# Layer 1 of the last two quarters emitted in turn

## The chip, the core and the metric

The kernel runs on one core of a Trainium2 chip. The metric is the device time of one launch in microseconds, as a median over runs. A profiled execution of the same program gives a span (first to last instruction) and the granted clock of TensorE. Engines: PE is TensorE, DVE is VectorE, ACT is ScalarE, POOL is GpSimd, SP issues most DMAs.

## The reference, cut to what matters

Two transformer layers on 1024 tokens (32 sequences of 32) of width 256, in float32. Each `_ref` is one block, and four residual sums join them:

```python
x = x + _L0_attn_ref(_L0_cond_ref(x, ...), ...)     # a mixing per sequence, then attention in 16 heads
x = x + _L0_ffn_ref(_L0_cond2_ref(x, ...), ...)     # gated feed-forward with low-rank adapters, then a second one
x = x + _L1_attn_ref(_L1_cond_ref(x, ...), ...)     # attention with a scale per sequence, then a linear-memory read
x = x + _L1_ffn_ref(_L1_cond2_ref(x, ...), ...)     # attention over a paged cache, then a mixture of 16 experts
```

The change is in the third line. `_L1_cond_ref` projects q, k and v, scales q, takes a causal softmax within each sequence of 32, multiplies by v and by `Wo`. `_L1_attn_ref` then forms `sigma_q = elu(q) + 1` from its own projection of that, and for each of four memory banks `sigma_q @ memories / clip(sigma_q . memory_norms)`; the banks are summed with softmax weights and multiplied by a last `Wo`. The block behind it begins with projections of q, k and v from the new x, an RMS norm of each head and a rotation by position; the new k and v are written into the paged cache before it is read.

## The kernel before

The 1024 tokens are worked on in four quarters of 256 (`NQ = 4`), with features on the partitions: a tile of a quarter is 128 x 2 x 256[...]. Stages in order: the layer 0 attention of each quarter; the feed-forwards of quarter 0; then, by the loop of lines 879 to 882, `layer1(q)` followed by `feed_forward(q + 1)`, which needs nothing of `layer1(q)`; `layer1(3)` comes last and has no feed-forward after it. Then weights of the last stages are loaded (lines 886 to 900), the paged attention gathers its rows (line 921, `kv<-rows_d`), and the experts follow.

The order in which the lines are written is not the order of the instructions: a scheduler places every instruction in its engine's queue, so that `layer1(q)` and `feed_forward(q + 1)` come out mixed with each other.[...] What may be open at the same time is set by tile pools. In PSUM: `mm` has two banks (projections), `tr` two, `sc` one (scores and norms), `ff` three (feed-forward alone). In SBUF each tag has its own buffers: `x1` four and `res` four (one a quarter), `QT`, `KT` and `AV` two each, `V` and `y` one each, `kb`, `sm`, `PT`, `th` and `h` two each.

`layer1(q)` is a chain. `mha` makes q, k and v (three banks of `mm` in turn, helper `products`, whose matmuls all have line 177), spreads V into the block-diagonal tile `vblk` (sixteen small copies, lines 393 and 395, half on DVE and half on ACT), and for each of two groups of 128 tokens: spreads K into `kb` (402), multiplies by q (409), adds the mask, takes the softmax (417 to 427), transposes (430), copies to `PT` (432), multiplies by `vblk` (436) and copies into `AV` (443). Then follow `Wo` and the copy to `cT` (779), the `lq` product and its `elu + 1` on DVE and ACT (786 to 788), the norms (791) and their reciprocal `rn` (799 to 801), the spread of `rn` to all rows by `esel` (811, 64 rows high) times `sq` (812, tile `t4`), the memories `mblk` and the copy to `comb` (817), the `lo` product, and `x3` (821). Last come k and v of the next block, rotated, written to DRAM by a DMA in SP's queue (846), and q, rotated into `qall`. `rotated` is a row of DVE operations with a Square and a Sqrt on ACT.

The gathers of line 921 wait until every row of `rows_d` is written. The tile `ew` (6 MB of expert weights, 895) lies in the place of the feed-forwards' weights; its load waits for the last of their products, `f_w_down`.

Of the kernel before, what the change touches and what calls it, by code (L numbers as in the profile page):

```python
# [18 lines left out]
F32 = mybir.dt.float32  # L19
# [5 lines left out]
P = 128  # L25
B, S, D = 32, 32, 256
NT = B * S
NG = NT // P
CH = 512
NCH = NT // CH  # L30

NQ, QG = 4, 2
QN = QG * P
# [88 lines left out]
def tile_layers(ctx: ExitStack, tc: tile.TileContext, i: dict, out: bass.AP):  # L122
    nc = tc.nc
    v, s, g_, te = nc.vector, nc.scalar, nc.gpsimd, nc.tensor
# [79 lines left out]
    with (  # L204
# [9 lines left out]
        def bank(pool=mm, tag="mm"):  # L214
            return pool.tile([P, 2, QN], F32, tag=tag, name=tag)

        def tok(tag, bufs=2, shape=(P, 2, QN)):
            return qp.tile(list(shape), F32, tag=tag, name=tag, bufs=bufs)

        late = {}
# [15 lines left out]
        with (  # L238
# [4 lines left out]
            for q in range(NQ):  # L243
                t = xp.tile([P, QG, D], F32, name=f"x0{q}")
# [49 lines left out]
            wa = {k: load_w(wp, i[f"L0_attn_W{k}"], f"wa_{k}") for k in "qkvo"}  # L294
# [37 lines left out]
            x0T, zT = [], []  # L332
# [34 lines left out]
                    s.copy(x0T[q][:, :, js], pt[:, 2:])  # L367


        def mha(zq, w, q_out, k_out, v_out):  # L370


            QT, KT, V, AV = tok("QT"), tok("KT"), tok("V", 1), tok("AV")
            for dst, k, put in ((QT, "q", q_out), (KT, "k", k_out)):
                ps = bank()
                products([(ps[:, m], ktiles(w[k], m, zq)) for m in range(2)])
                put(dst, ps)
            ps = bank()
            products(
                [  # L380
                    (ps[:, j], [(zq[:, k, j * P : (j + 1) * P], w["v"][:, k, :]) for k in range(2)])
                    for j in range(QG)
                ]
            )
            v_out(V, ps)

            V4 = V.rearrange("p g (hg h d) -> p g hg h d", hg=4, h=4)
            for b4 in range(4):
                for h4 in range(4):
                    dst = vblk[32 * h4 : 32 * h4 + 32, :, b4, :, 16 * h4 : 16 * h4 + 16]  # L390
                    src = V4[32 * b4 : 32 * b4 + 32, :, :, h4, :]
                    if h4 % 2:
                        v.tensor_copy(dst, src)  # L393
                    else:
                        s.copy(dst, src)
            for j in range(QG):
                js = slice(j * P, (j + 1) * P)
                ps = sc.tile([P, CH], F32, tag="sc", name="sc")
                for m in range(2):

                    kb = sp.tile([P, 4, 8, 32], F32, tag="kb", name="kb")
                    v.tensor_tensor(  # L402
                        kb,
                        KT[:, m, js].rearrange("p (b k) -> p b k", b=4).unsqueeze(2).broadcast_to([P, 4, 8, 32]),
                        m8.unsqueeze(1).unsqueeze(3).broadcast_to([P, 4, 8, 32]),
                        ALU.mult,
                    )
                    for b4 in range(4):
                        te.matmul(  # L409
                            ps[32 * b4 : 32 * b4 + 32, m * 256 : (m + 1) * 256],  # L410
                            lhsT=QT[:, m, j * P + 32 * b4 : j * P + 32 * b4 + 32],
                            rhs=kb[:, b4].rearrange("p h k -> p (h k)"),
                            start=True,
                            stop=True,
                        )
                sm = sp.tile([P, 16, 32], F32, tag="sm", name="sm")
                v.tensor_tensor(  # L417
                    sm, ps.rearrange("p (h k) -> p h k", k=32), C("causal").unsqueeze(1).broadcast_to([P, 16, 32]), ALU.add
                )
                mx = sp.tile([P, 16], F32, tag="mx", name="mx")  # L420
                v.tensor_reduce(mx, sm, AX.X, ALU.max)  # L421
                v.tensor_tensor(sm, sm, mx.unsqueeze(2).broadcast_to([P, 16, 32]), ALU.subtract)
                s.activation(sm, sm, AF.Exp)
                su = sp.tile([P, 16], F32, tag="su", name="su")
                v.tensor_reduce(su, sm, AX.X, ALU.add)
                v.reciprocal(su, su)
                v.tensor_tensor(sm, sm, su.unsqueeze(2).broadcast_to([P, 16, 32]), ALU.mult)
                pt = tr.tile([P, 4, P], F32, tag="tr", name="tr")
                for hg in range(4):
                    te.transpose(pt[:, hg], sm[:, 4 * hg : 4 * hg + 4, :].rearrange("p h k -> p (h k)"), ident)  # L430
                PT = sp.tile([P, 4, P], F32, tag="PT", name="PT")
                s.copy(PT, pt)
                av = tr.tile([P, 4, P], F32, tag="tr", name="tr")
                for b4 in range(4):
                    for hg in range(4):
                        te.matmul(  # L436
                            av[64 * (hg % 2) : 64 * (hg % 2) + 64, hg // 2, 32 * b4 : 32 * b4 + 32],
                            lhsT=vblk[:, j, b4, hg, :],
                            rhs=PT[:, hg, 32 * b4 : 32 * b4 + 32],
                            start=True,  # L440
                            stop=True,
                        )
                s.copy(AV[:, :, js], av[:, :2])
            return AV


        x1T = []
        for q in range(NQ):
# [9 lines left out]
            def v_out(dst, ps):  # L458
                v.tensor_tensor(dst, ps, bv.unsqueeze(1).broadcast_to([P, QG, D]), ALU.add)

            AV = mha(zT[q], wa, q_out, k_out, v_out)
            x1T.append(tok("x1", 4))
            ps = bank()
            products([(ps[:, m], ktiles(wa["o"], m, AV)) for m in range(2)])
# [298 lines left out]
        esel = C("esel", 64).rearrange("p (n a c) -> p n a c", n=4, a=2)  # L763


        def layer1(q):
            def q_out(dst, ps):
                v.tensor_tensor(
                    dst.rearrange("p m (b t) -> p m b t", t=S),
# [2 lines left out]
                    ALU.mult,  # L772
                )

            AV = mha(x2T[q], wa1, q_out, s.copy, s.copy)
            cT = tok("AV")
            ps = bank()
            products([(ps[:, m], ktiles(wa1["o"], m, AV)) for m in range(2)])
            s.copy(cT, ps)


            sq = tok("QT")
            ps = bank()
            products([(ps[:, m], ktiles(lq, m, cT)) for m in range(2)])
            e = sp.tile([P, 2, QN], F32, tag="sm", name="e")
            v.tensor_scalar(e, ps, 0.0, None, ALU.min)
            s.activation(e, e, AF.Exp)
            v.scalar_tensor_tensor(flat(sq), flat(ps), 0.0, flat(e), ALU.max, ALU.add)
            pn = sc.tile([P, CH], F32, tag="sc", name="sc")
            for m in range(2):  # L790
                te.matmul(
                    pn[32 * m : 32 * m + 32, :QN],
# [6 lines left out]
            v.tensor_scalar(rn, pn[:64, :QN], 1e-6, None, ALU.max)  # L799
            v.reciprocal(rn, rn)  # L800
            v.tensor_scalar(rn, rn, wcol, None, ALU.mult)
            comb = tok("KT")
            pc = bank()
            sums = []
            for m in range(2):
                pairs = []
                t4 = sp.tile([P, 4, QN], F32, tag="kb", name="t4")
                for b2 in range(2):
                    ps = bank()
                    for a in range(2):  # L810
                        te.matmul(ps[:, a], lhsT=esel[:, 2 * b2 + a, m, :], rhs=rn, start=True, stop=True)  # L811
                    v.tensor_tensor(
                        t4[:, 2 * b2 : 2 * b2 + 2], ps, sq[:, m].unsqueeze(1).broadcast_to([P, 2, QN]), ALU.mult
                    )
                sums.append((pc[:, m], [(mblk[:, m, bnk, :], t4[:, bnk]) for bnk in range(4)]))
            products(sums)
            s.copy(comb, pc)
            ps = bank()
            products([(ps[:, m], ktiles(lo, m, comb)) for m in range(2)])
            x3 = x3T[:, :, q * QN : (q + 1) * QN]  # L820
            done = v.tensor_tensor(x3, ps, x2T[q], ALU.add)
# [13 lines left out]
                v.tensor_copy(at[:, :, 4], ps[:, B : B + NG])  # L835


            gs = slice(QG * q, QG * q + QG)
            kvw = tok("V", 1, (P, QG, D))
            ps = bank()  # L840
            xg = [[x3[:, k, j * P : (j + 1) * P] for k in range(2)] for j in range(QG)]
            products([(ps[:, j], [(xg[j][k], wqkv[:, k, D:]) for k in range(2)]) for j in range(QG)])
            s.copy(kvw[:, :, P:], ps[:, :, P:])
            kd = kvw[:, :, :P].rearrange("p g (h a d) -> a p g h d", a=2, d=16)
            rotated(ps[:, :, :P].rearrange("p g (h d) -> p g h d", d=32), 4, 1, gs, [(kd[0], kd[1])])
            nc.sync.dma_start(new_rows[:, gs, :], kvw)
            ps = bank()
            products([(ps[:, j], [(xg[j][k], wqkv[:, k, :D]) for k in range(2)]) for j in range(QG)])
            qd = qall[:, gs].rearrange("p g h k (a d) -> h a p g k d", a=2)
            rotated(ps.rearrange("p g (h d) -> p g h d", d=32), 8, 0, gs, [(qd[h, 0], qd[h, 1]) for h in range(2)])  # L850

        def rotated(x, nh, j, gs, dst):


            shape = [P, QG, nh, 32]

            def tile_(tag):
                t = sp.tile([P, CH], F32, tag=tag, name="r" + tag)
                return t[:, : QG * nh * 32].rearrange("p (g h d) -> p g h d", g=QG, h=nh)

            sq = tile_("sm")
# [14 lines left out]
                v.tensor_tensor(dst0, ak[:, :, :, :16], bk_[:, :, :, 16:], ALU.subtract)  # L876
                v.tensor_tensor(dst1, ak[:, :, :, 16:], bk_[:, :, :, :16], ALU.add)

        for q in range(NQ):
            layer1(q)  # L880
            if q + 1 < NQ:
                x2T.append(feed_forward(q + 1))


    with tc.tile_pool(name="w1", bufs=1, reuse_waits="tile") as wp:
# [455 lines left out]
```

## Time and profile before

| | us |
|---|---|
| median of 3 runs | 724.82 (724.69 to 726.23) |
| profiled execution, own time | 742.99 |
| its span | 741.1 |
| PE busy in the span | 596.4 (80%) |
| DVE, ACT, POOL busy | 375.9, 182.9, 188.4 |
| mean granted clock of PE | 0.895 of full |
| last feed-forward ends | 440.2 |
| last rows of k and v issued | 501.5 |
| first gather of the paged attention | 504.55 |

Times on the axis of the span are from the first instruction. A busy PE counts matmuls whose ends are modelled, and each float32 matmul of the program shows as two records. The rows of the views name a line, an operation and its tiles without buffer numbers: `mm<-res,wb_q` is a matmul from a `res` tile and a weight into a bank of `mm`.

### The profile page before, as it was taken

To read this page: it belongs to the slowest core of one execution; us is meant where nothing else is said; L and a number is where in the kernel's file an instruction comes from. 1 tells how busy PE (TensorE), PEld (TensorE's weight loads), DVE (VectorE), ACT (ScalarE), POOL (GpSimd) and SP (SyncE) were. 2 spreads that over 40 slices of the span, in tenths; PEclk is the share of its full clock that TensorE was granted. 3 is DMA by queue.
4 is the path that set the end of the run, shared out by engine and by line. 5 is a ranking of instruction groups with operands and counts; after the bars stand their busy time and mean duration, and the time that the engine had idled before them with its cause. 6 is when DMAs were issued, how large, how long until landed. Compare 5 with 4: busy or idle time off the path is not lost.

```text
span 741.1 us, 9080 instructions
## 1 busy us (share of the span) xinstructions
PE 596.4 (80%) x3246; PEld 457.5 (62%) x3246; DVE 375.9 (51%) x874; ACT 182.9 (25%) x490; POOL 188.4 (25%) x274
## 2 busy tenths in 40 slices
PE   2649899997999989999899994674388899249990
PEld 1426677784877858788588882452266657136660
DVE  4583584699445364333734227223177747115553
ACT  1132222213212122210222103011266643102220
POOL 6213333204694000000000000005456200624541
PEclk9877899998899999999899996675599999759996
DMA  6984354300700000000000036003212000223325
GB/s 197 252 298 127 107 134 129 113 13 2 219 15 14 1 1 1 1 14 1 0 2 0 15 121 261 1 1 106 64 58 72 23 0 1 86 75 114 117 61 170
DMA packets 37452, 55.35 MB, mean 75 GB/s; under 512 B 8906, under 2 KB 29536, under 8 KB 36576
## 3 DMA queue, kind: packets, MB, share of 16 engines
q1 hardware_dynamic: 27549, 37.62, 15.9%
q0 software_dynamic: 5904, 15.40, 7.6%
q10 hardware_dynamic: 3955, 1.75, 0.9%
q8 instruction: 26, 0.43, 0.2%
q14 instruction: 18, 0.15, 0.1%
HBM read 38.56 MB, written 18.17 MB: 77 GB/s over the span
## 4 chain that ended last, share of the span: by engine, by line
PE 48%; issue 27%; DVE 15%; POOL 4%; DMA 3%; ACT 2%; another core or an unknown queue 1%; POOLq 0%; SPq 0%; ACTq 0%; DVEq 0%
PE ff L177 26%; PE mm L177 13%; POOL ys_d L1247 4%; DVE kb L402 4%; PE tr L436 3%; PE mm L811 3%; DVE vblk L393 2%; PE tr L430 1%; DVE sm L417 1%; DMA y<-ys_d 1%; PE sc L409 1%; PE mm L346 1%; DVE mx L421 1%; DMA adi<-in_itok_B 0%
## 5 line engine op out<-in xcount | busy, mean ns | idle before, releaser
L921 POOL DMA_INDIRECT kv<-rows_d,at x40 | 38.7, 968 | 283.6 <-DMA sh_g<-in_L_ffn_sWg 273.0
L501 DVE SCALAR_TENSOR_TENSOR th<-th,ff 128x512 f32<-128x512 f32 x32 | 21.9, 683 | 63.5 <-ACT th L500 63.5
L560 POOL COPY rr<-raw 88x256 f32<-88x256 f32 x64 | 27.9, 467 | 80.0 <-DMA rows_d<-rr 40.8
L409 PE MATMUL sc<-kb,QT 128*32 128x256 f32 x256 | 24.5, 459 | 23.2 <-DVE kb L402 12.3
L402 DVE TENSOR_TENSOR kb<-KT,con 128x1024 f32<-128x1024 f32 x32 | 38.7, 1227 | 8.2 <-ACT KT L456 4.5
L1247 POOL DMA_INDIRECT ys_d<-yb,xb x31 | 30.6, 986 | 44.5 <-DVE yb L1245 43.0
L177 PE MATMUL ff<-x,w_g 128*128 128x256 f32 x128 | 39.7, 429 | 0.0
L1232 PE MATMUL gu<-ew,xT 128*128 x124 | 34.4, 400 | 2.7 <-issue 2.7
L500 ACT ACTIVATE th<-ff 128x512 f32<-128x512 f32 x32 | 19.1, 596 | 69.4 <-PE ff L177 66.5
L177 PE MATMUL ff<-x,w_u 128*128 128x256 f32 x128 | 35.1, 385 | 0.0
L177 PEld LDWEIGHTS ff<-x,w_g 128*128 128x128 f32 x128 | 27.5, 219 | 6.1 <-issue 1.2
L987 PE MATMUL po<-PT,kv 128*128 128x256 f32 x64 | 18.6, 415 | 15.3 <-ACT PT L984 15.3
L177 PE MATMUL ff<-y,f_w_gate 128*128 128x256 f32 x128 | 30.9, 379 | 0.0
L177 PE MATMUL ff<-y,f_w_up 128*128 128x256 f32 x128 | 30.9, 379 | 0.0
L177 PE MATMUL ff<-h,d_Wd 128*128 128x256 f32 x128 | 30.1, 381 | 0.0
L1226 PE MATMUL xt<-ident,xb 128*128 128x128 f32 x62 | 11.9, 290 | 21.8 <-DMA xb<-xs_d 21.7
L502 DVE SCALAR_TENSOR_TENSOR h<-th,ff 128x512 f32<-128x512 f32 x32 | 21.7, 680 | 15.2 <-PE ff L177 14.9
L409 PEld LDWEIGHTS sc<-kb,QT 128*32 128x32 f32 x256 | 5.5, 116 | 37.7 <-DVE kb L402 19.3
L177 PE MATMUL ff<-h,f_w_down 128*128 128x256 f32 x128 | 28.3, 379 | 0.0
L969 ACT ACTIVATE sm<-sm,mx 128x160 f32<-128x160 f32 x64 | 26.7, 418 | 5.5 <-DVE mx L967 4.4
L1232 PEld LDWEIGHTS gu<-ew,xT 128*128 128x128 f32 x124 | 23.1, 199 | 7.0 <-issue 3.2
L955 PE MATMUL sc<-KT,qz 128*128 128x160 f32 x128 | 25.7, 339 | 1.4 <-issue 1.1
(334 smaller groups left out, 1346.0 us busy)
## 6 DMA issues: line engine op xcount, KB each, us to landing
ew<-in_L_ffn_W SPq DMA_DIRECT2D x1, 6144.0 KB
rows_d<-rr SPq DMA_DIRECT2D x32, 176.0 KB
xs_d<-none SPq DMA_DIRECT2D x1, 3999.0 KB
xb<-xs_d SPq DMA_DIRECT2D x31, 129.0 KB
x<-in_x SPq DMA_DIRECT2D x4, 256.0 KB
w_g<-in_L_cond_Wg SPq DMA_DIRECT2D x1, 1024.0 KB
w_u<-in_L_cond_Wu SPq DMA_DIRECT2D x1, 1024.0 KB
d_Wd<-in_L_cond_Wd SPq DMA_DIRECT2D x1, 1024.0 KB
```

What stands on the lines that cost most here:

```text
L177: mm_ = te.matmul(ps, lhsT=a, rhs=b, start=j == 0, stop=j == len(pairs) - 1)
L402: v.tensor_tensor(kb, KT[:, m, js].rearrange("p (b k) -> p b k", b=4).unsqueeze(2).broadcast_to([P, 4, 8, 32]), m8.unsqueeze(1).unsqueeze( ...
L409: te.matmul(ps[32 * b4 : 32 * b4 + 32, m * 256 : (m + 1) * 256], lhsT=QT[:, m, j * P + 32 * b4 : j * P + 32 * b4 + 32], rhs=kb[:, b4].rear ...
L436: te.matmul(av[64 * (hg % 2) : 64 * (hg % 2) + 64, hg // 2, 32 * b4 : 32 * b4 + 32], lhsT=vblk[:, j, b4, hg, :], rhs=PT[:, hg, 32 * b4 : 3 ...
L501: v.scalar_tensor_tensor(flat(t), flat(t), 1.0, flat(pg), ALU.add, ALU.mult)
L560: g_.tensor_copy(r[:, :, j].rearrange("p o g d -> p g o d"), raw[j].rearrange("p (g a o d) -> a p g o d", g=4, a=8, d=32)[a],)
L811: te.matmul(ps[:, a], lhsT=esel[:, 2 * b2 + a, m, :], rhs=rn, start=True, stop=True)
L921: got = g_.indirect_dma_start(out=kv[:, a, :], out_offset=None, in_=rows_d, in_offset=bass.IndirectOffsetOnAxis(ap=at[:, g, a : a + 1], ax ...
L955: te.matmul(ps[:, h, :], lhsT=q.qz[:, b, h].rearrange("p g t -> p (g t)"), rhs=q.KT[:, b, :], start=True, stop=True,)
L969: s.activation(sm[:, h], sm[:, h], AF.Exp, bias=mx[:, h : h + 1], accum_out=q.su[:, b, h : h + 1])
L1232: te.matmul(pg[:, :D], lhsT=xT[:, k * P : (k + 1) * P], rhs=w[:, k * D : (k + 1) * D], start=k == 0, stop=k == 1)
L1247: g_.indirect_dma_start(out=ys_d, out_offset=bass.IndirectOffsetOnAxis(ap=xb[:, D + 1 :].bitcast(I32), axis=0), in_=yb, in_offset=None, bo ...
```

## The change

`mha` and `layer1` become generators: `yield` cuts `layer1` into seventeen steps. A `Chain` says in which banks and tiles a layer works. The first chain is the old one. The second has its projections, scores and norms in the three `ff` banks, QT, KT and AV in the four buffers of `x1`, V in `y`, `kb` and `t4` in `h`, `sm` and `e` in `th`; `vblk`, `tr`, `PT` and the small tiles are shared. `emit` runs a generator for n steps, or to its end. Quarters 0 and 1 are emitted as before. Of the third quarter eight steps (all of `mha`) are emitted, then the last feed-forward, then both layers in turn, two steps of the last quarter for one of the third.

```diff
+        class Chain:
+            def __init__(self, sums=(mm, "mm"), scores=(sc, "sc"), names=None):
+                self.sums, self.scores, self.names = sums, scores, names or {}
+            def bank(self):
+                return bank(*self.sums)
+            def score(self):
+                pool, tag = self.scores
+                return pool.tile([P, CH], F32, tag=tag, name=tag)
+            def tok(self, tag, shape=(P, 2, QN)):
+                tag, bufs = self.names.get(tag) or (tag, 1 if tag == "V" else 2)
+                return tok(tag, bufs, shape)
+            def tile(self, tag, shape, name=None):
+                tag = self.names.get(tag) or tag
+                return sp.tile(list(shape), F32, tag=tag, name=name or tag)
+        first_chain = Chain()
+        second_chain = Chain(
+            (ff, "ff"),
+            (ff, "ff"),
+            {"QT": ("x1", 4), "KT": ("x1", 4), "AV": ("x1", 4), "V": ("y", 1), "kb": "h", "sm": "th"},
+        )
+        def emit(steps, n=None):
+            while n is None or n > 0:
+                try:
+                    next(steps)
+                except StopIteration as e:
+                    return e.value
+                n = n and n - 1
...
-        def mha(zq, w, q_out, k_out, v_out):
-            QT, KT, V, AV = tok("QT"), tok("KT"), tok("V", 1), tok("AV")
+        def mha(zq, w, q_out, k_out, v_out, ch=first_chain):
+            QT, KT, V, AV = (ch.tok(k) for k in ("QT", "KT", "V", "AV"))
...
-                ps = sc.tile([P, CH], F32, tag="sc", name="sc")
+                ps = ch.score()
...
-                    kb = sp.tile([P, 4, 8, 32], F32, tag="kb", name="kb")
+                    kb = ch.tile("kb", [P, 4, 8, 32])
...
-            AV = mha(x2T[q], wa1, q_out, s.copy, s.copy)
-            cT = tok("AV")
-            ps = bank()
+            AV = yield from mha(x2T[q], wa1, q_out, s.copy, s.copy, ch)
+            cT = ch.tok("AV")
+            ps = ch.bank()
...
-        for q in range(NQ):
-            layer1(q)
-            if q + 1 < NQ:
-                x2T.append(feed_forward(q + 1))
+        for q in range(NQ - 2):
+            emit(layer1(q))
+            x2T.append(feed_forward(q + 1))
+        one, two = layer1(NQ - 2), layer1(NQ - 1, second_chain)
+        emit(one, 8)
+        x2T.append(feed_forward(NQ - 1))
+        for _ in range(9):
+            emit(two, 2)
+            emit(one, 1)
+        emit(one)
+        emit(two)
```

In the changed program's queues the loads of `ew` and the constants stand in SP's order ahead of both late writes of rows, the last quarter's first and the third quarter's second.

The seventeen steps end behind: q and k; v and `vblk`; for each group of 128 tokens the softmax, the `PT` copy and the `AV` copy; the `cT` copy; `sq`; `rn`; `t4` of each half; `comb`; `x3`; the write of rows; q.

## The prediction

> **What bounds the kernel now.** I read the page first, for the slices in which TensorE stops being the bound.
>
> ```profile
> PE   2649899997999989999899994674388899249990
> DVE  4583584699445364333734227223177747115553
> PEclk9877899998899999999899996675599999759996
> ```
>
> A slice is 18.5 us. From slice 10 to 23 PE is nearly full: layer 1 of a quarter runs among the feed-forward of the next. Slices 24 to 27 (444 to 519 us) have PE at 0.4 to 0.7, DVE at 0.7 and then 0.2 to 0.3, and a granted clock of 0.5 to 0.7. There layer 1 of the last quarter stands alone. The stretch view gives its size (length; busy time of PE, weight loads, DVE, ACT, POOL with counts; granted clock; DMA):
>
> ```profile
> 376.17:402.65 26.48, 26.48 (x119) 21.10 (x118) 9.36 (x14) 4.18 (x8) 0.00 (x0) 1.00 0.00 1
> 402.65:440.21 37.56, 37.56 (x176) 33.06 (x175) 13.32 (x28) 6.76 (x12) 0.00 (x0) 1.00 0.09 28
> 440.21:501.45 61.24, 40.21 (x206) 28.84 (x204) 25.09 (x47) 11.54 (x25) 0.00 (x0) 0.73 0.26 104
> ```
>
> Up to 440.21, where the last feed-forward ends, PE is the bound at full clock. The 61.24 us after it are a chain of dependences: PE 40.2, DVE 25.1, ACT 11.5 take turns. The chain view shows the same matmuls hidden (third quarter, first four rows) and alone (last quarter):
>
> ```profile
> 376.54 1.73 PE mm L177 x8
> 387.74 1.92 PE mm L811 x8
> 392.21 3.65 PE mm L177 x16
> 399.39 3.64 PE mm L177 x16
> ...
> 464.81 3.79 PE mm L177 x8
> 476.82 7.16 PE mm L811 x16
> 483.98 6.39 PE mm L177 x16
> ```
>
> Eight records of L177 take 1.73 us hidden and 3.79 alone, L811 0.24 us a record against 0.45: the last quarter runs mostly at half clock. What ends the stage:
>
> ```profile
> 501.49 0.38 SPq L846 DMA_DIRECT2D rows_d<-V  x1
> ...
> 504.55 1.06 POOL L921 DMA_INDIRECT kv<-rows_d,at  x1 [273.01 <-DMA sh_g<-in_L_ffn_sWg]
> ```
>
> The gathers of the paged attention wait for the last key-value rows; from the issue of that write to the first gather are 3.06 us. Everything behind follows from there.
>
> **What the change takes away.** Up to the eighth step of the third quarter the order on every engine is the same. Then its remaining nine steps leave the feed-forward. On PE these are 72 records in bank mm and four of L791. In the chain view their pieces add up to 1.73 + 1.81 + 0.56 + 1.92 + 1.92 + 3.65 + 1.80 + 3.64 = 17.0 us. The stretch says it another way: of 26.48 us, 42 records are the feed-forward's own, at 0.2155 us 9.05; 17.4 are left, with the small gaps at each change. I take 17.4. What is left there is PE-bound: two matmul groups of a feed-forward step take 24 x 0.2155 = 5.2 us on PE, against ACT 0.60 and DVE 0.69 + 0.69, and three banks. So the last feed-forward ends 17.4 us sooner. The Sqrt and Tanh table loads in it (1.28 us each at 402.02 and 406.13) leave it too; PE ran over them at full clock, so I count them at nothing.
>
> **What it puts in their place.** I walk the changed order engine by engine, with the durations of this trace, on the old time axis; the 17.4 come off at the end. "One" is the third quarter, "two" the last. PE's granted clock must be known first; I take half from 455.4 to 479.7 (argued below).
>
> Two's projections are as before. One's Wo (1.73) goes in ahead of two's scores, partly where PE waited for kb. One's cT copy queues on ACT behind two's eight vblk copies (2.44) and comes at 449.3, so one's lq product runs 449.3 to 451.1. On DVE one's e 0.69, QT 0.66, rn 0.42 + 1.75 + 0.35 stand inside two's softmax: 3.9 us, of which some 1.2 fall into its waits. Second softmax group done: 461.4 against 458.7, +2.7. On PE three of one's L811 groups (4 records, 1.79 each at half clock) stand between two's transposes and value products; 1.0 more is late: those products end at 468.1 against 464.4, +3.7. Two's Wo ends at 473.3 (+4.7). One's fourth L811 group (1.79) and the lq product at half clock (3.44; before it happened to run at full, 2.0) give 478.6, +7.3. Two's QT is then ready at 480.7, but 8 + 4 of one's mblk records are queued ahead of its norm product: 483.1, +9.0. The reciprocal chain keeps it: 485.7. Now the 32 records of L811 and mblk run at full clock, 16 x 0.23 + 16 x 0.216 and their waits, 7.8 us instead of 13.6: 493.5, +3.1. x3 of two: 496.9, +3.1. The key-value products of both end at 499.8 against 495.8, +4.0. The rotation is DVE's: two's steps come first, and one's write goes last, at 508.2 against 501.4, +6.8. Second-half steps of q (5.4 us of DVE) come after the write and before the first transpose of gathered rows (6.0 us after it), so they stay hidden, with 0.6 us to spare; if it fails, so much is lost.
>
> Sum: -17.4 + 6.8 = -10.6 us.
>
> **DMA and queues.** The third quarter's write of rows (L846, issued at 407.32) now stands last in SP's queue, behind con3, wo2, wr, ew and two's write. The 6 MB of ew wait for PE's last f_w_down product, which comes 17.4 us earlier as well (440.62 before); the DMA share falls from 0.91 to 0.12 at 456, so they are landed long before two's write at 505.0 on this axis. Nothing else in that queue waits for a late event. The gathers on POOL now wait for two late writes where one was late before. The sh_ loads stay behind it; their first user comes at 620 us. Second-chain tiles lie in x1, y, h and th, unread once the feed-forward is done; its three ff banks are free from QT's evacuation on, so I cost these waits at 0, at most 0.7 each (one L812). ACT has one table load at the end, as before.
>
> **The clock[...].** The trace shows steps of 3.4 us (busy PE is the first figure after the length, granted clock the third from the end):
>
> ```profile
> 448.55:451.95 3.40, 0.64 (x8) 0.19 (x8) 3.35 (x6) 0.30 (x2) 0.00 (x0) 0.99 0.99 422
> 451.95:455.36 3.41, 1.08 (x8) 0.20 (x8) 2.81 (x5) 0.63 (x1) 0.00 (x0) 0.50 1.06 461
> 465.60:469.00 3.40, 2.99 (x7) 1.82 (x6) 0.00 (x0) 0.38 (x1) 0.00 (x0) 0.50 0.00 0
> 479.25:482.65 3.40, 3.40 (x10) 2.65 (x9) 1.37 (x3) 0.00 (x0) 0.00 (x0) 0.50 0.00 0
> 482.65:486.10 3.45, 3.45 (x9) 2.35 (x8) 1.05 (x2) 0.00 (x0) 0.00 (x0) 0.50 0.00 0
> 486.10:489.50 3.40, 3.40 (x9) 2.68 (x9) 0.00 (x0) 0.00 (x0) 0.00 (x0) 0.51 0.00 0
> 489.50:492.90 3.40, 2.73 (x12) 1.84 (x11) 0.00 (x0) 0.59 (x1) 0.00 (x0) 1.00 0.04 3
> ```
>
> A step with 0.64 us of PE loses the clock. Full-height matmuls for 2.99 us (465.60) bring it back; two wholly busy steps do not, filled by L811 with its 64 rows and then by L811 and mblk mixed; the third, mblk alone, does. (Transposes and value products, 2.93 us busy from 458.80, did not either.)[...] By the rows, L811, narrow value products and transposes do not count in full; the first pure step is Wo or lq and mblk of one: back between 473 and 481, sum -14.7 to -10.6. I take the row, at its late end, since Wo (3.4 us) fills one step only if it falls on it exactly. That it cools at all: between 452.3 and 457.4 PE has only 0.5 us to do.
>
> **Rivals.** First, the clock comes back early[...], or is never lost: -16.4, or -21.0 with the walk at full clock throughout. For it: more work in the same time. Against it: the two busy steps at 0.50.
>
> Second, the slower end: half clock stays on to the key-value products, because the two chains, waiting for each other, never fill one step with full-height matmuls. Its place is L811 and mblk of both quarters, 64 records at 0.40 to 0.45 us in place of 0.22. Lasting until 490 it leaves -7.0, until 500 -2.4; it decides at 505 on this axis, where the sum is zero; lasting to the gathers it gives +5.5, or 730.3. Against it: 486.10 to 489.50 shows mblk alone reopening the clock, and the merged queue has mblk directly behind the lq product.
>
> Third, the write of one is late for DVE alone: the four rotations (12.4 us) in series after the products instead of woven in. The walk has PE ahead of DVE already from 499 on; without any overlap some 2 to 3 us more, -8. That the interleaving is undone by the scheduler is excluded: the order on PE has one's Wo ahead of two's scores.
>
> **How the numbers follow.** The profiled execution took 742.99 us, 1.89 beside its span of 741.1; it would become 732.4. The median of the runs is 724.82, 2.4% lower, but a saving of 10.6 scaled by that is 10.3, so I carry it over whole: 714.2 us. Chances: late return of the clock 0.56, the same with the rotations in series 0.06; early return 0.22, no loss 0.05; half clock to 490 or beyond, 0.11, of which 0.04 end slower and 0.03 within 0.2% (1.45 us, about what a measurement of this kernel can tell from no change). The range leaves out the uncooled -21 and the end beyond about -4.5: 706.5 to 720.5. Faster 0.93, same 0.03, slower 0.04.
>
> **What would show it.** The gap from the last f_w_down product to the write of V grows from 61 to about 68 us; f_w_down ends near 423; PE's clock is 0.5 from about 438 to 462 of the new span; the write starts at about 491; DVE is busy without a break in the last 8 us ahead of it. I am wrong if PE stalls inside the feed-forward in the freed places, if the clock returns before Wo of two, or if a stage behind the gathers changes its length.

## The result, and the profile after

| | before | changed |
|---|---|---|
| median of four runs, us | 725.53 (724.69 to 727.31) | 715.59 (713.54 to 717.3) |
| profiled execution, own time, us | 742.99 | 716.79 |
| its span, us | 741.1 | 715.0 |
| mean granted clock of PE | 0.895 | 0.912 |

The ratio of the times is 0.9857, with a 95% interval of 0.9834 to 0.9879: 9.9 us less. Forecast were 714.2 us, and 10.6 less. All ratios here leave out executions more than 1.5% above the fastest of their kernel, which is one: the profiled execution of the changed kernel on the first chip below.

The two spans differ by 26.1 us, far more than the times. The profiles seem to come from different chips: from the first gather to the first attention output the one before has 36.4 us and the one after 27.2, and the same program has 36.1 on the first chip below and 26.7 on the third. In the four profiles of the first chip and in the one before, ACT sits idle for 5.9 to 8.9 us ahead of its first `PT` copy there, and in the others it does not; what it waits for, the traces don't show. Below, lengths of stretches are compared within one profile, and kernels with others that ran on the same chip.

Three rows of the page, slices of 17.9 us in tenths:

```profile
PE   2748999997999989999899997964788999069990
DVE  4865595699445354443541355454577727025553
PEclk9967899998899999999989995995999989669996
```

Before, four slices from 24 on had PE at 4, 6, 7, 4 and the clock at 5 to 7. Now the late stage has one slice with the clock down at 5, slice 24 (429 to 447 us, PE at 7); slices 25 and 26 have PE at 9 and 6 and the clock at 9. Slice 27 (PE 4, clock 5) begins at 482.6, behind the last write.

Line numbers move with the edit: L402 is now L443, L430 and L436 are L472 and L479, L811 is L857, L846 is L895, L921 is L980. In the stretch view (length; busy PE, weight loads, DVE, ACT, POOL with counts; clock; DMA) the first row of each kernel begins at the third quarter's first `kb` copy and ends where SP issues the load of `ew`, at the end of the last `f_w_down` product. The second goes from there to the last write of rows. Before:

```profile
354.83:440.62 85.79, 82.36 (x438) 67.08 (x438) 37.57 (x69) 17.66 (x35) 0.00 (x0) 0.96 0.04 13
440.62:501.49 60.87, 39.80 (x204) 28.46 (x202) 25.13 (x47) 11.54 (x25) 0.00 (x0) 0.73 0.26 104
```

After, with the part behind the first gather as a third row:

```profile
348.82:417.24 68.42, 64.95 (x362) 54.06 (x362) 25.37 (x43) 11.65 (x25) 0.00 (x0) 0.95 0.04 12
417.24:480.74 63.50, 52.39 (x280) 38.88 (x278) 34.02 (x65) 14.86 (x32) 0.00 (x0) 0.86 0.26 104
483.74:715.00 231.26, 165.09 (x819) 118.41 (x819) 116.44 (x321) 75.78 (x263) 92.99 (x119) 0.88 0.24 73
```

The 76 PE records that the change moves leave the first stretch (438 to 362) and come back in the second (204 to 280). The first shrinks by 17.37 us. The second takes them in for 2.63: its PE time grows by 12.6, and PE's idle time falls from 21.1 to 11.1. Together they are 14.74 us shorter.

The end of the stage in SP's queue:

```profile
417.24 0.33 SPq L954 DMA_DIRECT2D ew<-in_L_ffn_W  x1
478.00 0.38 SPq L895 DMA_DIRECT2D rows_d<-y  x1
480.74 0.38 SPq L895 DMA_DIRECT2D rows_d<-V  x1
```

SP issued them in the order of its queue. The last quarter (tile `y`) writes first, the third (tile `V`) 2.7 us later; the first gather starts at 483.74, 3.00 us behind the second write (3.06 before). The chain view of the same stage:

```profile
437.81 2.00 PE mm L857 x4
...
444.71 2.00 PE mm L857 x4
446.72 3.29 PE ff L177 x8
450.00 1.06 PE mm L857 x4
451.06 1.92 PE ff L177 x8
...
459.43 3.65 PE ff L857 x16
463.08 3.67 PE ff L177 x16
```

Tiles `mm` are the third quarter, `ff` the last. Four L857 take 2.00 us at half clock and 1.06 at full. The last quarter's sixteen L857 and sixteen L177 of the memories, which took 7.16 and 6.39 us when it ran alone, now take 3.65 and 3.67. Where the clock changed is seen in windows cut near the changes (clock third from the end):

```profile
430.00:435.00 5.00, 1.52 (x8) 0.86 (x8) 5.00 (x11) 1.63 (x3) 0.00 (x0) 0.74 0.57 246
...
437.70:446.60 8.90, 8.90 (x51) 6.00 (x48) 1.38 (x2) 1.33 (x3) 0.00 (x0) 0.50 0.00 0
446.60:450.00 3.40, 3.40 (x10) 2.48 (x9) 0.69 (x1) 0.00 (x0) 0.00 (x0) 0.58 0.00 0
450.00:476.50 26.50, 25.57 (x113) 19.88 (x112) 10.45 (x18) 6.07 (x12) 0.00 (x0) 1.00 0.01 1
```

PE is busy for 1.52 us of the 5 from 430 to 435, and the clock falls to 0.50 at 432.38. From 437.70 PE is busy without any gap for 8.90 us, with transposes, value products and L857, and the clock stays at 0.50. L857 has a height of 64, that is, it sums over 64 rows (its form in the view is `64*128`), where `Wo` and the memories sum over 128 (`128*128`), called full height here. Of these windows only the one that holds the last quarter's `Wo`, matmuls of full height, ends with the clock open.

In this profile the granted clock changes at 432.38, 449.44, 480.16 and 497.23, that is, 5, 9 and 5 times 3.41 us apart, and in all fourteen profiles of this document the time between two changes is a whole multiple of 3.41 us. So below the time on both sides of a change is cut into steps of that length. Here the clock opened at 449.44, at the end of the step

```profile
446.03:449.44 3.41, 3.41 (x9) 2.26 (x8) 0.69 (x1) 0.00 (x0) 0.00 (x0) 0.50 0.00 0
```

of which `Wo` (from 446.72 in the chain) fills 2.7 us and L857 the rest.

### The profile page after: what moved, and what is told of

It reads as the page before. It is cut to its first block, busy times and chain, and to the rows that moved or that the text cites. A ratio compares the mean times of both kernels' runs of the same rounds, so it can differ in the third digit from the quotient of the medians.

```text
span 715.0 us, 9081 instructions
## 1 busy us (share of the span) xinstructions
PE 589.6 (82%) x3246; PEld 454.1 (64%) x3246; DVE 377.1 (53%) x874; ACT 180.3 (25%) x488; POOL 195.9 (27%) x274
## 4 chain that ended last, share of the span: by engine, by line
PE 54%; DVE 20%; issue 9%; POOL 7%; ACT 5%; DMA 3%; POOLq 0%; ACTq 0%; DVEq 0%; SPq 0%
PE ff L177 29%; PE mm L177 9%; POOL ys_d L1306 4%; DVE kb L443 3%; PE tr L479 3%; DVE vblk L433 2%; PE po L1046 2%; PE mm L857 2%; ACT sm L1028 2%; DVE sm L1022 1%; POOL xs_d L1236 1%; PE tr L472 1%; PE mm L1231 1%; PE sc L1014 1%; DMA y<-ys_d 1%
## 5 line engine op out<-in xcount | busy, mean ns | idle before, releaser
L980 POOL DMA_INDIRECT kv<-rows_d,at x40 | 39.4, 984 | 268.9 <-DVE rPT L919 258.3
L545 DVE SCALAR_TENSOR_TENSOR th<-th,ff 128x512 f32<-128x512 f32 x32 | 21.9, 684 | 71.3 <-ACT th L544 71.3
L604 POOL COPY rr<-raw 88x256 f32<-88x256 f32 x64 | 33.8, 563 | 79.3 <-DMA rows_d<-rr 41.1
L177 PE MATMUL ff<-x,w_g 128*128 128x256 f32 x128 | 39.5, 429 | 0.0
L443 DVE TENSOR_TENSOR kb<-KT,con 128x1024 f32<-128x1024 f32 x28 | 34.1, 1237 | 7.0 <-ACT KT L500 4.5
L450 PE MATMUL sc<-kb,QT 128*32 128x256 f32 x224 | 21.6, 464 | 18.8 <-DVE sm L458 8.9
L177 PE MATMUL ff<-x,w_u 128*128 128x256 f32 x128 | 34.8, 384 | 0.0
L177 PEld LDWEIGHTS ff<-x,w_g 128*128 128x128 f32 x128 | 27.5, 219 | 6.0 <-issue 1.2
L546 DVE SCALAR_TENSOR_TENSOR h<-th,ff 128x512 f32<-128x512 f32 x32 | 21.8, 681 | 17.9 <-PE ff L177 17.6
L177 PE MATMUL ff<-y,f_w_gate 128*128 128x256 f32 x128 | 30.9, 379 | 0.0
L177 PE MATMUL ff<-y,f_w_up 128*128 128x256 f32 x128 | 30.9, 379 | 0.0
L177 PE MATMUL ff<-h,d_Wd 128*128 128x256 f32 x128 | 30.1, 381 | 0.0
L177 PE MATMUL ff<-h,f_w_down 128*128 128x256 f32 x128 | 28.3, 379 | 0.0
L1028 ACT ACTIVATE sm<-sm,mx 128x160 f32<-128x160 f32 x64 | 26.7, 418 | 4.3 <-DVE mx L1026 3.1
L177 PEld LDWEIGHTS ff<-h,d_Wd 128*128 128x128 f32 x128 | 24.0, 190 | 4.0 <-issue 0.8
L177 PEld LDWEIGHTS ff<-y,f_w_gate 128*128 128x128 f32 x128 | 24.3, 190 | 3.3
L177 PEld LDWEIGHTS ff<-y,f_w_up 128*128 128x128 f32 x128 | 24.3, 190 | 3.3
```

The costliest lines, as they stand in the source:

```text
L177: mm_ = te.matmul(ps, lhsT=a, rhs=b, start=j == 0, stop=j == len(pairs) - 1)
L443: v.tensor_tensor(kb, KT[:, m, js].rearrange("p (b k) -> p b k", b=4).unsqueeze(2).broadcast_to([P, 4, 8, 32]), m8.unsqueeze(1).unsqueeze( ...
L450: te.matmul(ps[32 * b4 : 32 * b4 + 32, m * 256 : (m + 1) * 256], lhsT=QT[:, m, j * P + 32 * b4 : j * P + 32 * b4 + 32], rhs=kb[:, b4].rear ...
L545: v.scalar_tensor_tensor(flat(t), flat(t), 1.0, flat(pg), ALU.add, ALU.mult)
L546: v.scalar_tensor_tensor(flat(h[:, f : f + 2]), flat(t), 0.5, flat(pu), ALU.mult, ALU.mult)
L604: g_.tensor_copy(r[:, :, j].rearrange("p o g d -> p g o d"), raw[j].rearrange("p (g a o d) -> a p g o d", g=4, a=8, d=32)[a],)
```

## The experiments

My theory had three parts: the moved steps save what PE spent on them in the feed-forward; the merged stage absorbs them because PE waited there; and what it costs depends on how long the half clock lasts, which, as I supposed, the 64-row spread of `rn` prolongs. The rivals: the gain comes from the second chain's banks alone; the turn-taking does not matter, since leaving the feed-forward is all; something behind the gathers changes. Twelve runs in three groups, each group on one chip; a ratio is to the kernel before on the same chip. Stretches, in us, of one profiled execution each: feed-forward is from the third quarter's first `kb` copy to the last matmul that reads `f_w_down` (0.4 us ahead of the end of that product, which is used above), late stage from there to the last write, rear from the first gather to the end, half is the time at half clock within the late stage (counted in windows of 0.5 us, so up to 1 us too long).

| run | feed-forward | late stage | half | both stretches | rear |
|---|---|---|---|---|---|
| first chip: kernel before | 83.9 | 63.3 | 41.0 | 147.2 | 240.5 |
| changed kernel | 67.0 | 66.7 | 25.5 | 133.7 | 240.9 |
| changed, spread of full height | 66.6 | 58.8 | 7.5 | 125.5 | 238.8 |
| before, spread of full height | 83.6 | 57.4 | 24.0 | 141.1 | 236.4 |
| second chip: old order, second banks | 83.9 | 63.3 | 41.0 | 147.2 | 229.7 |
| steps moved, not in turn | 66.3 | 80.5 | 34.5 | 146.8 | 229.8 |
| eleven steps ahead | 71.3 | 61.2 | 10.0 | 132.4 | 228.8 |
| eleven steps, full height | 70.9 | 57.5 | 3.5 | 128.5 | 229.0 |
| third chip: kernel before | 85.4 | 61.3 | 33.0 | 146.7 | 227.7 |
| changed kernel | 66.2 | 64.6 | 17.0 | 130.9 | 232.9 |
| changed, full height | 67.4 | 59.4 | 10.0 | 126.8 | 228.4 |
| same, third quarter first in a turn | 66.4 | 59.3 | 13.5 | 125.8 | 227.3 |

**The kernel before, on the first chip.** No edit.

> The kernel before once more, for the lengths of its stretches in a second execution. Theory (the change is worth what the two stretches around the last feed-forward give): from the third quarter's first kb copy to the load of ew 85.8 us within 0.3; from there to the last write of rows 58 to 62, depending on where the clock's steps fall; the stretch ahead of it (354.8) and the one behind the first gather (236.6) differ from the first profile by several us, since they differ by execution and not by kernel. Rival (the profile's saving of 14.7 us in these stretches is the usual one, and the median shows only 9.9 because something behind the gathers got longer): the stretch behind the gather is again near 236.6.

One execution, 745.18 us; 741.92 is the median of the runs of the kernel before in this group. It gives the stretches that the next three are compared with. Cut at the load of `ew`, as the expectation has them, they are 84.3 (85.8 within 0.3 was expected) and 62.9 (58 to 62): even one program's late stage varies with the clock, 41 us at half instead of 33.5 in the first profile. `Wo` fell across two steps of the clock here, with 2.6 and 2.7 us, and did not open the clock.

**The changed kernel, on the first chip.** No edit.

> The changed kernel once more, with five rounds. Theory: ratio 0.984 to 0.988; feed-forward stretch 68.4 within 0.3, merged stretch 61 to 68 by the step in which the clock comes back (63.5 in the first profile, where it came back in Wo of the last quarter). Rival: stretches as in the first profile, and the stretch behind the gather 4 to 5 us longer than that of the kernel before in the same call.

727.15 us, ratio 0.9791 (0.9738 to 0.9844), below the 0.984 to 0.988 expected. The profiled execution was the longest of the six, 732.96, so its row of the table is read for the place of the clock and not for the time. In it the clock came back 38.5 us into the late stage, where the forecast had it (39), and the stage took 66.7 against the forecast's 68. Both stretches are 13.5 shorter than in the run before it. The feed-forward lost 16.9. The rear is no longer (240.9 against 240.5), so the expectation's rival fails on this chip. Why the clock came back one place later than in the first profile is seen in the chain and in the steps:

```profile
450.50 3.71 PE ff L177 x8
454.21 2.00 PE mm L857 x4
456.21 3.33 PE ff L177 x8
```

```profile
448.77:452.19 3.42, 3.42 (x8) 2.31 (x8) 0.69 (x1) 0.14 (x1) 0.00 (x0) 0.50 0.00 0
452.19:455.60 3.41, 3.41 (x9) 2.19 (x8) 0.00 (x0) 0.59 (x1) 0.00 (x0) 0.50 0.00 0
455.60:459.01 3.41, 3.41 (x9) 2.33 (x8) 0.69 (x1) 0.00 (x0) 0.00 (x0) 0.50 0.00 0
```

`Wo` (from 450.50) lies across two steps with 1.7 and 2.0 us, beside L857, and does not open the clock. The `lq` product behind it has 2.8 us of the third step, and the clock is open from 459.01.

**The spread of `rn` at full height, in the changed kernel.** The constant `esel` is read with all its 128 rows, and `rn` gets 64 rows of zeros below it, set once, so the values are the same:

```diff
+        rnz = [wp.tile([P, QN], F32, name=f"rnz{j}") for j in range(2)]
+        for t in rnz:
+            g_.memset(t[64:], 0.0)
-        esel = C("esel", 64).rearrange("p (n a c) -> p n a c", n=4, a=2)
+        esel = C("esel").rearrange("p (n a c) -> p n a c", n=4, a=2)
-            rn = sp.tile([64, QN], F32, tag="rn", name="rn")
+            rn2 = rnz[q % 2]
+            rn = rn2[:64]
-                        te.matmul(ps[:, a], lhsT=esel[:, 2 * b2 + a, m, :], rhs=rn, start=True, stop=True)
+                        te.matmul(ps[:, a], lhsT=esel[:, 2 * b2 + a, m, :], rhs=rn2, start=True, stop=True)
```

> The changed kernel with the spread of rn by esel 128 rows high in place of 64: the same number of matmuls of the same length, the added rows are zeros on both sides. Theory (64-row matmuls do not count in full for the clock): the clock comes back within the L857 groups, at 441 to 446 on the axis of the changed kernel's profile instead of 449.7; the merged stretch is 60 to 62 us, and the time is 1.5 to 4 us below that of the changed kernel (ratio to before 0.980 to 0.985). Rival[...]: clock and time as with 64 rows, within 0.5 us.

721.51 us, ratio 0.9725 (0.9688 to 0.9761): further than the 0.980 to 0.985 expected, with a late stage of 58.8 where 60 to 62 was. The half clock lasts 7.5 us. Number and order of the matmuls are the same, only their height differs.

**The same edit in the kernel before.**

> The kernel before with the spread of rn by esel 128 rows high in place of 64, nothing else. Theory: the clock of the lone last quarter comes back at 480 to 483 instead of 489.3, so that 6 to 8 records of L811 and the 16 of mblk run at 0.22 us in place of 0.40 to 0.45: 4 to 5 us less, ratio 0.993 to 0.995. Rival[...]: within 0.5 us of the kernel before.

732.78 us, ratio 0.9884 (0.9842 to 0.9925): 9.1 us less, more than the 4 to 5 expected. The late stage accounts for 5.9 of it; the rest lies ahead of it and behind it (240.5 to 236.4 in the rear), where the two single profiles scatter by as much. I can't say what of that is the edit's.

**The second chain's banks and tiles in the old order.** Nothing is moved:

```diff
-        for q in range(NQ - 2):
+        for q in range(NQ - 1):
             emit(layer1(q))
             x2T.append(feed_forward(q + 1))
...
+        emit(layer1(NQ - 1, second_chain))
```

> One part of the change alone: quarters in the old order (third quarter whole, then the last feed-forward, then the last quarter alone), but the last quarter works in the second chain's banks and tiles. Theory (the gain is the third quarter's steps leaving the feed-forward for idle engines): feed-forward stretch as before (84 to 86), merged stretch 58 to 63 as before, ratio to before 0.995 to 1.002. Rival (three banks in place of two pay by themselves): merged stretch 4 us or more shorter than before, ratio below 0.994.

728.38 us against 726.2, ratio 1.0033 (1.0012 to 1.0054). The rival "banks alone" is out: they save nothing and may cost 2 us (the two stretches are as before, 147.2).

**The nine steps moved, but the two layers one after the other.**

```diff
         emit(one, 8)
         x2T.append(feed_forward(NQ - 1))
-        for _ in range(9):
-            emit(two, 2)
-            emit(one, 1)
         emit(one)
         emit(two)
```

> The other part: eight steps of the third quarter, the last feed-forward, then the rest of the third quarter emitted whole and the last quarter whole behind it, not in turn. The scheduler still mixes them, with the third quarter first. Theory (what pays is that the steps stand beside other work, the turn is of little account): feed-forward stretch 67 to 68.5, merged stretch within 3 us of the changed kernel's 63.5 to 66.3, ratio to before 0.976 to 0.988. Rival (the turn by turn order is what overlaps them): merged stretch 72 us or more, ratio at or above 0.995.

730.13 us, ratio 1.0044 (1.0024 to 1.0063). I had expected the opposite, 0.976 to 0.988, since I held the turn to be of little account; the rival came true. The feed-forward gives up just as much (66.3), and all of it is lost again: the late stage takes 80.5. SP's queue of this kernel and its stretches, cut at the third quarter's write:

```profile
452.21 0.36 SPq L895 DMA_DIRECT2D rows_d<-V  x1
454.16 0.41 SPq L950 DMA_DIRECT2D ew<-in_L_ffn_W  x1
495.34 0.38 SPq L895 DMA_DIRECT2D rows_d<-y  x1
```

```profile
414.80:452.20 37.40, 30.63 (x138) 21.79 (x136) 25.07 (x47) 9.54 (x22) 0.00 (x0) 0.86 0.00 1
452.20:495.30 43.10, 30.35 (x144) 22.72 (x144) 13.00 (x27) 8.01 (x14) 0.00 (x0) 0.72 0.43 171
```

The third quarter's chain is finished first, 37.4 us into the stage, and its write leads the one of the last quarter by 43 us. For those 43 us the last quarter is alone again at a clock of 0.72, as it was before. What pays is that the two waits overlap, not that the steps leave the feed-forward. (The load of `ew` stands behind the first write here and starts at 454.16; the rear is no longer for it, 229.8 against 229.7 in the run before this.)

**Eleven steps ahead of the feed-forward instead of eight**, six turns left:

```diff
-        emit(one, 8)
+        emit(one, 11)
         x2T.append(feed_forward(NQ - 1))
-        for _ in range(9):
+        for _ in range(6):
```

> One size changed: eleven steps of the third quarter stay among the last feed-forward instead of eight, so that cT, the lq product, the norms and rn are made there, and six steps go in turn. Theory: feed-forward stretch 4.1 us longer than with eight (71 to 72.5), since PE is full there; the merged stretch loses 3.9 us of DVE inside the softmax and has L857 groups ready for PE's idle time: 57 to 62. Sum equal to the changed kernel's or up to 4 us better. Rival (it is PE's moved work alone that counts): 4 us back, ratio to before 0.984 to 0.99.

715.48 us, ratio 0.9858 (0.9838 to 0.9878). This is the changed kernel's ratio, and both expectations allow it. The feed-forward keeps 5.1 us more than the changed kernel on the third chip (71.3 against 66.2), and the late stage is 3.4 shorter. Of the two cuts tried neither is better.

**Eleven steps, full height.** Both edits above.

> The same with the spread of rn by esel 128 rows high in place of 64 (added rows are zeros). Theory (full-height matmuls in PE's idle time hold or bring back the clock): merged stretch 54 to 58, ratio to before 0.964 to 0.974. Rival: no better than the changed kernel with full-height rows (merged 58.4).

710.53 us, ratio 0.9799 (0.9777 to 0.982): 5.0 less than without the full height, in the direction of the theory. This pair shows most plainly what height did to the clock in these runs, because the last quarter's sixteen spread matmuls run alone here behind a loss of the clock. Steps of the run before, 64 rows high:

```profile
457.08:460.49 3.41, 3.01 (x7) 2.46 (x8) 0.95 (x2) 0.00 (x0) 0.00 (x0) 0.50 1.00 432
460.49:463.90 3.41, 3.41 (x9) 2.63 (x9) 1.38 (x2) 0.00 (x0) 0.00 (x0) 0.50 0.86 365
```

and of this one, 128 rows high:

```profile
456.24:459.65 3.41, 2.80 (x7) 2.29 (x8) 1.12 (x3) 0.00 (x0) 0.00 (x0) 0.50 0.84 360
459.65:463.07 3.42, 3.42 (x18) 3.01 (x17) 2.08 (x3) 0.00 (x0) 0.00 (x0) 1.00 1.05 450
```

Two steps with 3.01 and 3.41 us of 64-row matmuls left the clock at half; one with 2.80 us of the padded ones was followed by full clock, from 459.65.

The late stage is 57.5, as expected, but the ratio expected was 0.964 to 0.974. The feed-forward (70.9) still carries the 5 us of the extra steps, and the two stretches together, 128.5, are no shorter than those of the changed kernel at full height (126.8 on the third chip).

**The kernel before and the changed one, on a third chip.** No edits; they test the rear.

> The kernel before against itself: ratio within 0.003 of 1. From the third quarter's first kb copy to the last write of rows 145 to 148 us, of which 61 to 64 behind the last f_w_down product.

> The changed kernel, in one call with the other three. Theory (17 us come off the feed-forward, and 3 to 6 come back behind it, by the step in which the clock returns): from the first kb copy to the last write 131 to 135 us; ratio to before 0.980 to 0.987. Rival (part of the saving is lost behind the gathers): that stretch is 131 to 135 but the time of the execution behind the first gather is 3 us or more longer than in the kernel before of this call.

726.42 us, ratio 1.0 (0.9985 to 1.0015), and 716.26, ratio 0.986 (0.9833 to 0.9886). Both stretches together lose 15.8 us, but the rear grows by 5.2 (227.7 to 232.9), as the rival said. Of that, 3.3 are in the router, from the last attention output to the first row sent to the experts (26.0 to 29.3). Its pieces in the chain view, of the kernel before:

```profile
595.72 3.48 PE rt L1070 x32
599.20 7.00 PE mm L1172 x32
```

and of the changed one:

```profile
577.92 4.17 PE rt L1129 x32
582.09 9.66 PE mm L1231 x32
```

The same 64 matmuls take 3.4 us more. Steps of 3.41 us show the clock there. The kernel before:

```profile
594.07:597.49 3.42, 3.42 (x23) 2.50 (x21) 0.00 (x0) 1.15 (x2) 0.00 (x0) 1.00 0.02 5
597.49:600.90 3.41, 3.41 (x25) 3.20 (x25) 1.17 (x4) 0.58 (x2) 0.00 (x0) 1.00 0.00 0
```

The changed one:

```profile
577.10:580.51 3.41, 3.41 (x28) 2.94 (x26) 0.00 (x0) 0.59 (x1) 0.00 (x0) 1.00 0.02 5
580.51:583.92 3.41, 3.41 (x13) 3.05 (x14) 0.87 (x3) 0.00 (x0) 0.00 (x0) 0.50 0.00 0
583.92:587.34 3.42, 3.42 (x10) 2.70 (x9) 1.73 (x6) 0.95 (x3) 0.00 (x0) 0.50 0.00 0
```

PE is busy all the time in both, at full clock in one and at half in the other. In the changed kernel the clock is lost at 580.51, at the end of a step that PE filled (3.41 us). The matmuls of that step, by form:

```profile
L1129 PE MATMUL rt<-wr,oT 128*128 128x16 f32 x26 | 3.1, 262 | 0.0
L192 PE MATMUL sc<-AVT,wo 128*128 128x512 f32 x2 | 1.0, 592 | 0.0
```

The router's 32 records of `rt` move 16 columns each and take about 3.6 us. Of the step 577.10 to 580.51 they have 2.75 us; in the kernel before they are spread over two steps, with 1.9 and 1.7. No edit touches this stage, and the fourteen profiles fall into two groups. In ten of them 2.5 us or more of one step were `rt`, the clock was lost at its end for one step or two, and the router took 27.6 us (six profiles) or 29.3 (four, among them all three of the changed kernel and the kernel before on the first chip); in the other four no step had more than 2.4, the clock was kept, and the router took 26.0 at most (among them the kernel before on the third chip). So in these profiles the loss goes with how the steps fall on this row of narrow matmuls. No run shifted them on purpose, and why a kernel gets the place that it gets stays open.

**The changed kernel with full height, on the third chip.** The edit is that of the first chip.

> The changed kernel with the spread of rn 128 rows high (added rows are zeros), in one call with the changed kernel. Theory: 4 to 8 us below it (first kb copy to last write 125 to 129 us), since the clock comes back 10 us or more earlier. Rival: its advantage in the earlier call was the chip's scatter, within 2 us of the changed kernel here.

707.55 us, ratio 0.9737 (0.9716 to 0.9758), 8.7 less than the changed kernel, a little more than the 4 to 8 expected. Its windows cut at the changes of the clock, and its chain there:

```profile
413.00:430.00 17.00, 13.62 (x86) 10.23 (x86) 11.33 (x21) 5.35 (x13) 0.00 (x0) 1.00 0.82 335
430.00:440.10 10.10, 7.83 (x52) 5.83 (x52) 6.62 (x12) 2.17 (x4) 0.00 (x0) 0.51 0.15 61
440.10:474.50 34.40, 29.20 (x158) 23.46 (x156) 16.11 (x33) 7.33 (x15) 0.00 (x0) 1.00 0.03 8
```

```profile
436.14 2.01 PE mm L861 x4
438.14 0.85 PE tr L472 x4
439.00 1.59 PE mm L861 x4
440.59 1.06 PE tr L479 x32
441.64 1.06 PE mm L861 x4
442.70 1.73 PE ff L177 x8
```

With the spread (L861 here) at full height the clock is back at 440.34, during its second group, ahead of the last quarter's second value products (1.06 us instead of 1.85) and of its `Wo` (1.73 instead of 3.29 in the changed kernel). Of the 8.7 us some 4.1 show in the two stretches and 4.5 in the rear, 1.7 of these in the router.

**The third quarter first in each turn**, with full height:

```diff
         for _ in range(9):
-            emit(two, 2)
             emit(one, 1)
+            emit(two, 2)
```

> As the run before it, but in each turn the step of the third quarter goes ahead of the two steps of the last. Theory (the end of the stage is the two rotations in series on DVE, the last write being the third quarter's): the third quarter's rotation moves into the last quarter's products, its write comes before the last quarter's, and the stretch is 1 to 3 us shorter. Rival (the stage is set by the last quarter's softmax, into which the third quarter's DVE work is pushed): 0 to 3 us longer.

706.7 us, ratio 0.9737 (0.9713 to 0.9761): neither the 1 to 3 us less of the theory nor clearly the rival's more. The third quarter's write does come first now, 54.0 us into the stage, but the last quarter's comes at 59.3, where the later one stood anyway. No difference that this tells; which of the two is put first decides nothing.

The best version is thus the changed kernel with the spread at full height: 2.6% under the kernel before on the third chip, where the change alone gives 1.4%.

## Why the prediction came close, step by step

**Feed-forward -17.4: right.** Measured -17.4, -16.9 and, on the third chip, -19.2. What was left stayed bound by PE (64.95 of 68.42 us busy), no bank wait came in its place, and losing the Sqrt and Tanh loads (1.28 us each) changed nothing that shows.

**The walk up to `Wo` of the last quarter: right.** Put on the old axis (plus 23.38, the difference of the two `f_w_down` starts), the last quarter's second softmax ends at 461.0 (walked: 461.4), its value products at 468.1 (468.1), its `Wo` at 473.4 (473.3).

**Late stage +6.8: the mis-sized term, +2.6 in this profile.** The step that failed is "I take the row, at its late end, since Wo (3.4 us) fills one step only if it falls on it exactly". It need not fill it: 2.7 us of `Wo` beside 0.7 of L857 were enough here (2.7 alone were not, in the kernel before on the first chip), and the prediction's own row at 465.60 has 2.99. The clock was back at 473 on the old axis, the early end of what I gave, and not at 479.7. From there on everything ran 2 to 4 us ahead of the walk: `lq` ended at 476.4 instead of 478.6, the memories at 490.1 instead of 493.5, the key-value products at 496.4 instead of 499.8. The rotations then took 7.7 us instead of 8.4, and DVE had 5.96 of the last 8.00 us, not all. That makes 4.1. Which end came went with how the steps fell: in the run on the first chip `Wo` lay across two, the clock came back at the late end, and the stage took 66.7 of the 68 walked. The working had the case, "-14.7"; I gave it the lesser place. Over the three pairs of kernels the two stretches lost 14.7, 13.5 and 15.8.

**The clock, by the rows: right.** In the changed kernel 8.90 us of gapless work (437.70 to 446.60) left the clock at 0.50, as the two busy steps of the prediction's rows had. The pair with eleven steps settles the part of L811 in this program: a step of 3.41 us filled by 64-row matmuls alone left the clock at 0.50, one with 2.80 us of the same matmuls padded to 128 opened it. The four pairs agree in direction, half clock 41.0 to 24.0, 25.5 to 7.5, 10.0 to 3.5 and 17.0 to 10.0 us; the sizes are single executions, and two of one kernel differ by 8 us (41.0 and 33.0). What the narrow value products and transposes do to the clock was not tried by itself.

**Queues and tiles at 0: right.** The write to the first gather stayed at 3.0, the second chain's banks cost nothing in the stretches (147.2 as before), and `ew` began 17 us earlier than before (counted from the third quarter's first `kb` copy) and delayed no write.

**Rear unchanged: wrong on the third chip.** The prediction named this as what would make it wrong. It took 5.2 us back, 3.3 of them in the router, where the clock was lost in one kernel and kept in the other; the remaining 2 us are spread over several stages by less than the profiles scatter. On the first chip both kernels lost the clock in the router, the rear stayed, and the ratio was 0.9791 (0.9738 to 0.9844), where it is 0.986 here. So the rear is the likely reason that the time fell by 9.8 on this chip, and by 9.9 in the result, although the two stretches fell by about 15. This rests on one pair of profiles: their spans differ by 13.9 us and the medians by 9.8, since the kernel before had its longest execution profiled. The closeness of 714.2 to 715.59 is then in part luck: about 4 us too little gained in the late stage and about 5 lost behind it have opposite signs.

**Rivals.** Early return of the clock (-16.4) stays excluded by the 8.90 us at 0.50. Half clock to the key-value products and the rotations in series did not occur: full clock lay on all of 450 to 476.5, and the writes came 2.7 us apart. That turn-taking, not the move alone, carries the gain lies in the walk, though I did not believe it when I wrote the series run's expectation; that run showed it: without the turns the time is 0.4% above the kernel before.

## What to carry to other kernels

A chain of dependences that stands alone costs its waits (21.1 us of PE's time here, 11.1 after the change); give it a second independent chain in turn, with its own banks and tiles, and take that one out of a stage where the engine is full. Moving the work there without interleaving it gained nothing here (730.13 us against 726.2). When such a stage runs at half clock, look for matmuls of few rows in it, and try padding them with zeros: in the four kernels tried here the two stretches lost 4 to 8 us by it and the time 5 to 9, beside 10 to 15 for the reordering.

## What the hardware showed that I had not expected

- Rows of zeros made PE faster here: the same matmuls in the same order, 128 rows high instead of 64, opened the clock with 2.80 us of a step where 3.41 us of the 64-row ones had not. In the changed kernel on one chip the half clock went from 17.0 to 10.0 us and the time from 716.26 to 707.55, about half of it in the two stretches.
- PE lost the clock at the end of a step that it filled (577.10 to 580.51, 3.41 us busy): in ten of the fourteen profiles the clock went to 0.50 behind a step of 3.41 us that held 2.5 us or more of matmuls of 16 columns, and one unchanged stage took 27.6 or 29.3 us instead of 26.0.
- Chips differ for one program, and in one place: 741.92 us on the first, 726.06 on the third, of which 9 to 10 us lie between the first gather and the first attention output (about 36 against 27 us).
